# Ordering attention keys by blocks of sixteen heads, most of them inside the first chunk of a graph network on one NeuronCore

## The chip, the cores and the metric

The kernel runs on one core of one Trainium2 chip. The metric is the device time of one execution in microseconds; lower is better. Engines are named as in the profile: PE (matrix products), DVE (vector engine), ACT (activations), POOL (GpSimd), SP (the engine that issues most transfers here). SPq in the profile is SP's queue of transfers.

## The reference

There are N = 3327 nodes with 128 features, a dense weighted adjacency matrix `adj` of 3327 x 3327, and four layers, each a normalisation, a ReLU, a graph layer and a residual sum. The change touches the first layer alone, an attention with 128 heads of 8 elements over all nodes, in which `adj` is added twice to the scores:

```python
q = (x @ Wq.T).reshape(d, n, h)          # d = 128 heads, n = 3327, h = 8
k = (x @ Wk.T).reshape(d, n, h)
v = (x @ Wv.T).reshape(d, n, h)
a = jnp.einsum('dnh,dmh->dnm', q, k) * scale
a = a + spatial_encoding + edge_encoding  # both are adj
a = jax.nn.softmax(a, axis=2)
out = jnp.einsum('dnm,dmh->dnh', a, v)
```

So 128 score matrices of 3327 x 3327 are made, exponentiated and multiplied with the values. The other three layers multiply `adj` and its transpose with 128 features per node.

## The kernel before, in words

**Prologue.** x is normalised and transposed, q, k and v are projected (L345). The raw k goes to `kraw_d`, element by element (eight elements, each for all heads), q split into a high and a low half (fp32r and the rest) to `qS_d`, v to `v_d`. Four "squares" of `adj`, 128 columns each, are turned into `adjT` with the maxima of its rows (class `Square`, L268 and after: `load` reads four strips of rows into the tile `rows`, `turn` transposes them on DVE at L288 into the tile `cols`, `largest` at L292 takes maxima, `store` writes `cols` to `adjT` at L295, `gather` at L299 and `back` at L304 pass the maxima through DRAM, `finish` adds them to the bound).

**Ordering the keys.** `k_halves(e)` (L412) is called eight times among the projections of v (L426 to L436), once for each of the eight elements. It loads element e of all 128 heads (L415), and for even and odd tiles of nodes makes the high half on ACT (L420) and the low half on DVE (L421), reading with a stride of 26 elements, and stores both to `kS_d` (L423). `kS_d` has, for each half, element and head, the nodes in the order in which the attention loop wants its tiles. The prologue is scheduled by the framework; from L599 on, the program's order is each engine's order.

**The attention loop.** There are 7 chunks c of up to 476 queries, 32 groups g of 4 heads in each, and 13 pairs q of node tiles in each group; a pair has the running number u. The order is written out by hand in the loop at L796 in slots i, four for a pair. In a slot stand ACT's exponentials (`exps`, L666 and L669), DVE's seeds of the score banks (`seed`, L645: a tile of `adjT` less the shift is put in a PSUM bank before PE adds the scores of four heads to it one after the other), PE's products (`scores` L654, `values` L713), and, for pairs 0, 2, 5, 7 and 10 of each group, an exponential made on DVE instead of ACT (`hand_exp`, L691 to L697). A score bank becomes free when ACT has read it, and the seed of a pair three or four pairs on waits for that.

Loads for the next group are issued by SP in the program's order: at pair 1 the keys (`load_k`, sixteen transfers into `KT`, L551), the first head's q (`load_q`, L562 and L564) and the values (`load_v`, L575); at pairs 3, 5 and 7 POOL writes the negated q of one head into the next head's rows (`negate_q`, L570) and SP loads the next head's q over a part of it; at pair 8 POOL spreads the values (L580) and reads the keys once (`all_here`, L584), on which the group's first score waits. SP runs ahead of the other engines as far as buffers are free.

Other work is put behind a pair with `plan(u, f, ...)`: in slot 4u, after the first pieces of `hand_exp` and before the seeds and loads of that pair, f issues its instructions. `plan_squares(c)` so spreads the squares of chunk c + 1 over chunk c: one strip in a group, loaded at pair 0, turned at pairs 4 and 9, its maxima at pair 12; each square ends with `gather`, `back`, `finish` and `store` at pairs 0, 1, 7 and 8 of the next group. The tiles `cols` and `rows` have one buffer each.

After the loop the outputs are normalised and projected, and the other three layers follow.

## Time and profile before

| What | us |
|---|---|
| median of 3 runs | 10980.69 (10976.75 to 10984.85) |
| profiled execution | 10981.96 |
| its span | 10980.2 |
| prologue, up to the loop's first instruction | 419.2 |
| first score of the loop (L654) | 461.2 |
| first and last store copy of the loop (L721) | 518.2 and 10170.7 |
| granted TensorE clock over the span | 0.985 |

The profiled execution is 1.3 us above the median. The page gives each engine's busy time over the whole span, which mixes the prologue (0 to 419 us), the loop (to about 10180 us) and the last three layers; what is true of one isn't true of the other. In a timeline row stand the start, the busy time, the engine, the line, the operation, what is written from what is read, the number of instructions merged into the row, and in brackets how long the engine was idle before and who ended it. For SPq a row is the time that issuing took, not that of the transfer; the time to landing has to be read from the engine that waits for it.

### The profile page before, as it was taken

What the parts mean: (1) busy time and instruction counts of PE and PEld (TensorE: products, weight loads), DVE (VectorE), ACT (ScalarE), POOL (GpSimd) and SP (SyncE); (2) the same over time, 40 slices, a digit from 0 to 9 for tenths busy, and PEclk for the clock granted to TensorE, in tenths of its full rate; (3) what the DMA queues carried; (4) which work ended last, traced back from release to release, by engine and by line L of the source; (5) the groups of instructions that cost most, each with busy time, mean ns of one, the idle gap of its engine ahead of it and who ended that gap; (6) DMA issues with size and microseconds to landing.
All of it is one profiled execution on the core that took longest, in us unless ns stands there. A gap on an engine that the chain in (4) does not pass through costs nothing. (4 is left out here: it accounts for less than half of the span.)

```text
span 10980.2 us, 204474 instructions
## 1 busy us (share of the span) xinstructions
PE 10533.5 (96%) x72876; PEld 3435.7 (31%) x72876; DVE 8487.1 (77%) x13503; ACT 10033.1 (91%) x13789; POOL 1529.1 (14%) x2477
## 2 busy tenths in 40 slices
PE   4599999999999999999999999999999999999889
PEld 2133333333333333333333333333323333333544
DVE  5588887888878887788887888878877777777655
ACT  3599999999999999999999999999999999999330
POOL 5011111111111111111111111111111111111101
PEclk7799999999999999999999999999999999999999
DMA  8766566565566565565556565565556555554668
GB/s 250 250 99 97 94 96 113 93 98 96 89 118 97 93 97 88 106 98 97 90 95 119 94 96 93 95 119 95 87 93 98 96 95 86 82 88 71 206 233 281
DMA packets 695339, 1256.98 MB, mean 114 GB/s; under 512 B 195218, under 2 KB 555049, under 8 KB 691244
## 3 DMA queue, kind: packets, MB, share of 16 engines
q1 hardware_dynamic: 644044, 1114.42, 55.7%
q0 software_dynamic: 50272, 129.37, 4.3%
q8 instruction: 587, 9.62, 0.4%
q14 instruction: 436, 3.57, 0.2%
HBM read 1096.53 MB, written 146.60 MB: 113 GB/s over the span
## 5 line engine op out<-in xcount | busy, mean ns | idle before, releaser
L666 ACT ACTIVATE e<-S 128x952 f32<-128x952 f32 (+1 forms) x9024 | 8357.9, 1099 | 36.7 <-PE S L654 29.4
L713 PE MATMUL po<-e,VA 128*9 128x476 f32 (+1 forms) x46592 | 5737.5, 564 | 33.0 <-DVE OS L721 12.3
L645 DVE TENSOR_TENSOR S<-a,shb 128x476 f32<-128x476 f32 (+1 forms) x5824 | 3937.9, 676 | 1447.6 <-ACT e L666 1059.4
L654 PE MATMUL S<-QS,KT 64*128 64x476 f32 (+1 forms) x22176 | 4528.6, 445 | 79.7 <-DMA a<-adjT 28.4
L654 PEld LDWEIGHTS S<-QS,KT 64*128 64x128 f32 x22176 | 2073.7, 184 | 5100.5 <-issue 1301.3
L669 ACT ACTIVATE e<-S 128x476 f32<-128x476 f32 (+1 forms) x4128 | 2467.5, 711 | 1.1 <-PE S L654 0.6
L695 DVE SCALAR_TENSOR_TENSOR e<-e,h 128x476 f32<-128x476 f32 (+1 forms) x2240 | 1497.8, 669 | 77.0
L713 PEld LDWEIGHTS po<-e,VA 128*9 128x9 f32 x46592 | 691.0, 88 | 1606.6 <-issue 1488.1
L570 POOL TENSOR_SCALAR QS<-QS 128x476 fp32r<-128x476 f32 (+1 forms) x672 | 485.6, 723 | 4312.1 <-DMA QS<-qS_d 2612.2
L725 POOL DMA_DIRECT2D oT_d<-OS x896 | 470.5, 530 | 3668.8 <-DVE OS L721 3625.5
L691 DVE TENSOR_SCALAR h<-S 128x476 f32<-128x476 f32 (+1 forms) x1120 | 728.0, 650 | 300.9 <-PE S L654 296.5
L697 DVE SCALAR_TENSOR_TENSOR e<-e,EA 128x476 f32<-128x476 f32 (+1 forms) x1120 | 759.6, 678 | 0.0
L695 DVE SCALAR_TENSOR_TENSOR e<-h 128x476 f32<-128x476 f32 (+1 forms) x1120 | 743.1, 663 | 0.0
L1107 PE MATMUL pu<-strip,y 128*128 128x512 f32 (+2 forms) x1456 | 600.5, 566 | 31.7 <-DVE y L968 14.8
L654 PE MATMUL S<-QZ,KT 64*128 64x476 f32 (+1 forms) x1120 | 493.4, 441 | 11.9 <-DVE S L645 10.5
L1107 PEld LDWEIGHTS pu<-strip,y 128*128 128x128 f32 (+1 forms) x1456 | 271.9, 191 | 305.8 <-issue 272.1
L1111 DVE TENSOR_REDUCE deg<-strip 128x1 f32<-128x1536 f32 (+1 forms) x104 | 193.8, 1881 | 63.7 <-DMA strip<-adjT 44.1
L580 POOL COPY VA<-VR 128x832 f32<-128x832 f32 x224 | 242.3, 1082 | 0.0
L654 PEld LDWEIGHTS S<-QZ,KT 64*128 64x128 f32 x1120 | 205.1, 183 | 92.2 <-DVE S L645 52.4
L288 DVE STREAM_TRANSPOSE cols<-rows 128x416 f32<-128x416 f32 x208 | 204.5, 988 | 30.3 <-DMA rows<-in_adj_dram 22.6
L1060 ACT COPY uT<-pu 128x512 f32<-128x512 f32 (+1 forms) x21 | 11.1, 555 | 222.6 <-PE pu L1107 222.6
L721 DVE COPY OS<-po 128x476 f32<-128x476 f32 (+1 forms) x224 | 146.3, 653 | 87.3 <-PE po L713 87.3
(255 smaller groups left out, 1958.6 us busy)
## 6 DMA issues: line engine op xcount, KB each, us to landing
KT<-kS_d SPq DMA_DIRECT2D x1792, 208.0 KB
KT<-kS_d SPq DMA_DIRECT2D x1792, 104.0 KB
VR<-v_d SPq DMA_DIRECT2D x224, 416.0 KB
QS<-qS_d SPq DMA_DIRECT2D x3072, 14.9 KB
QS<-qS_d SPq DMA_DIRECT2D x1536, 29.8 KB
adjT<-cols SPq DMA_DIRECT2D x26, 1664.0 KB
a<-adjT SPq DMA_DIRECT2D x156, 238.0 KB
strip<-adjT POOLq DMA_DIRECT2D x39, 895.5 KB, 5.1
```

The source lines that it names most:

```text
L570: nc.gpsimd.tensor_scalar(QS[b][:, j + 1, :w], QS[b][:, j, :w].bitcast(F32), -1.0, 0.0, op0=ALU.mult, op1=ALU.add)
L580: nc.gpsimd.tensor_copy(VA[(c * NG + g) % 2][:, :, :, 0:H], v.rearrange("p j (t e) -> p t j e", e=H))
L645: touch(u, [r], nc.vector.tensor_tensor(bank(u, r), adj_of[c][2 * q + r][:, :w], shift_of[c][:, :w], op=ALU.subtract))
L654: x = nc.tensor.matmul(bank(u, r), KT[b][64 * r:64 * r + 64, max(0, j - 1), q * P:(q + 1) * P], q_s[64 * r:64 * r + 64, :w], start=hand an ...
L666: touch(u, (0, 1), nc.scalar.activation(e[:, :, :w], S[:, odd:even + 1, :w], AF.Exp, scale=2.0))
L669: touch(u, [r], nc.scalar.activation(e[:, 1 - r, :w], bank(u, r), AF.Exp, scale=2.0))
L691: touch(u, [1], nc.vector.tensor_scalar(s, bank(u, 1), EXP_ARG, None, op0=ALU.mult))
L695: nc.vector.scalar_tensor_tensor(e, s if k == 3 else e, EXP_C[k], s, op0=ALU.add, op1=ALU.mult)
L697: nc.vector.scalar_tensor_tensor(e, e, EXP_C[0], EA[pairs[u][2]][:, :w], op0=ALU.add, op1=ALU.mult)
L713: nc.tensor.matmul(po[32 * j:32 * j + H + 1, :w], VA[k % 2][:, 2 * pairs[v][2] + of, j, :], e_of[v, j][:, 1 - of, :w], start=(q == 0 and r ...
L725: nc.gpsimd.dma_start(oT_d[:, d * N + c * CW:d * N + c * CW + w], o[32 * j:32 * j + H + 1, :w])
L1107: nc.tensor.matmul(ps[:, :k], y[:m, t, :], s[:m, c * 4 * P - c0:c * 4 * P - c0 + k], start=(t == 0), stop=(t == NT - 1))
```

## The change

Keys are ordered by blocks of 16 heads with all eight elements (16 x 8 = 128 rows) instead of by elements with all heads. Block 0 is ordered in the prologue, at the third pair of value tiles. Blocks 1 to 7 are ordered in the loop's first chunk: block b from the third pair of group 4(b - 1) on; it holds the keys that are loaded from pair 1 of group 4b - 1 on. There the high half is made by DVE and the low half by POOL, a half of the nodes' tiles at a time, in the tiles `cols` and `rows` of the squares. The four squares of chunk 1 move to the second half of these blocks, two strips to a group. Ahead of the loop, the first group's q of all four heads is loaded at once and negated in rows of 32, with the shift and four adj tiles ahead of the keys; values and the other adj tiles come after the keys. (The branch for scores without a bound gets the remaining blocks too; it doesn't run.)

```diff
+    def k_rows(b):
+        return bass.AP(tensor=kraw_d.tensor, offset=kraw_d.offset + KB * b * N, ap=[[N, KB], [GP, H], [1, N]])
...
-            if t0 >= 10:
-                k_halves(t0 // 2 - 5)
+            if t0 == 4:
+                k_block(0, a2)
...
-                if c + 1 < NC and (g, q) == (0, 0):
+                if c and c + 1 < NC and (g, q) == (0, 0):
                     plan_squares(c)
...
+            class Keys:
...
+                def load(self):
+                    raw = e_t.tile([P, NT, P], F32, name="cols").rearrange("p t n -> p (t n)")
+                    nc.gpsimd.memset(raw[:, N:NP], 0.0)
+                    nc.sync.dma_start(raw[:, :N], k_rows(self.b))
+                    self.of = raw.rearrange("d (p q r) -> d r q p", q=NQ, r=2)
+
+                def high(self, r, q0, q1):
+                    self.part = e_t.tile([P, 7 * P], F32, name="rows")[:, :(q1 - q0) * P]
+                    nc.vector.tensor_copy(self.part.rearrange("d (q p) -> d q p", p=P).bitcast(F32R),
+                                          self.of[:, r, q0:q1, :])
+                    k_store(self.b, 0, r, q0, self.part)
+
+                def low(self, r, q0, q1):
+                    part = self.part.rearrange("d (q p) -> d q p", p=P)
+                    nc.gpsimd.tensor_tensor(part.bitcast(F32R), self.of[:, r, q0:q1, :], part, op=ALU.subtract)
+                    k_store(self.b, 1, r, q0, self.part)
+
+            def plan_keys():
+                for b in range(1, HEADS // KB):
+                    u, keys = 4 * (b - 1) * NQ, Keys(b)
+                    plan(u + 2, keys.load)
+                    for at, r, h in ((5, 0, 0), (9, 0, 1), (14, 1, 0), (21, 1, 1)):
+                        plan(u + at, keys.high, r, 7 * h, 7 + 6 * h)
+                        plan(u + at + 2, keys.low, r, 7 * h, 7 + 6 * h)
+                    if b <= squares_of(1) - squares_of(0):
+                        sq = Square(e_t, squares_of(0) + b - 1)
+                        for j in range(4):
+                            v = u + 26 + 6 * j + j // 2
+                            plan(v, sq.load, j)
+                            plan(v + 3, sq.turn, j, 0)
+                            plan(v + 5, sq.turn, j, 1)
+                            plan(v + 5, sq.largest, j)
+                        for k, f in ((25, sq.gather), (25, sq.store), (27, sq.back), (33, sq.finish)):
+                            plan(u + 26 + k, f)
...
-            v0 = load_v(0, 0)
-            load_k(0, 0)
-            load_q(0, 0, 0)
-            shift_of[0] = load_shift(0)
-            for j in range(3):
-                negate_q(0, 0, j)
-                load_q(0, 0, j + 1)
+            for j in range(4):
+                load_q(0, 0, j)
+            shift_of[0] = load_shift(0)
+            adj_of[0] = [load_adj(0, t) for t in range(4)]
+            load_k(0, 0)
+            v0 = load_v(0, 0)
+            adj_of[0] += [load_adj(0, t) for t in range(4, NT)]
+            for j in range(3):
+                for r0 in (32 * (1 - j % 2), 64 + 32 * (1 - j % 2)):
+                    nc.gpsimd.tensor_scalar(QS[0][r0:r0 + 32, j + 1, :CW], QS[0][r0:r0 + 32, j, :CW].bitcast(F32),
+                                            -1.0, 0.0, op0=ALU.mult, op1=ALU.add)
             spread_v(0, 0, v0)
             here[0] = all_here(0, 0)
-            adj_of[0] = [load_adj(0, t) for t in range(NT)]
```

`k_block(b, pool)`, used for block 0, does what `k_halves` did, with `k_rows(b)` as its source; `k_store` writes the sixteen heads' rows of one half into `kS_d`.

More of the change, by code (lines that the diff above doesn't have):

```diff
@@ L39 @@
 NG = HEADS // 4
+KB = P // H
 HALF_SCALE = 0.5 * D ** -0.5
@@ L275, in load @@
                 self.cols = self.pool.tile([P, NT, P], F32, name="cols")
-            self.rows = self.pool.tile([P, KW], F32, name="rows")
+            self.rows = self.pool.tile([P, 7 * P], F32, name="rows")[:, :KW]
             n0 = self.s * P + 32 * j
@@ L320, in square, with k_store, k_block @@
         return q
+    def k_rows(b):
+        return bass.AP(tensor=kraw_d.tensor, offset=kraw_d.offset + KB * b * N, ap=[[N, KB], [GP, H], [1, N]])
+    def k_store(b, i, r, q0, half):
+        m = half.shape[-1]
+        nc.sync.dma_start(bass.AP(
+            tensor=kS_d.tensor, offset=kS_d.offset + (i * H * HEADS + KB * b) * NP + (r * NQ + q0) * P,
+            ap=[[NP, KB], [HEADS * NP, H], [1, m]]), half)
+    def k_block(b, pool):
+        raw = pool.tile([P, NP], F32, name="st_q0")
+        nc.gpsimd.memset(raw[:, N:NP], 0.0)
+        nc.sync.dma_start(raw[:, :N], k_rows(b))
+        of = raw.rearrange("d (p q r) -> d r q p", q=NQ, r=2)
+        for r in range(2):
+            hi = pool.tile([P, NQ, P], F32R, name="st_k0")
+            lo = pool.tile([P, NQ, P], F32R, name="st_q1")
+            nc.scalar.copy(hi, of[:, r])
+            nc.vector.tensor_tensor(lo, of[:, r], hi.bitcast(F32), op=ALU.subtract)
+            for i, half in enumerate((hi, lo)):
+                k_store(b, i, r, 0, half.bitcast(F32).rearrange("d q p -> d (q p)"))
     def head_rows(tensor):
@@ L410, in bound_scores @@
             return wide
-        def k_halves(e):
-            raw = a2.tile([P, NP], F32, name="st_q0")
-            nc.gpsimd.memset(raw[:, N:NP], 0.0)
-            nc.sync.dma_start(raw[:, :N], head_rows(kraw_d[e]))
-            of = raw.rearrange("d (p q r) -> d r q p", q=NQ, r=2)
-            for r in range(2):
-                hi = a2.tile([P, NQ, P], F32R, name="st_k0")
-                lo = a2.tile([P, NQ, P], F32R, name="st_q1")
-                nc.scalar.copy(hi, of[:, r])
-                nc.vector.tensor_tensor(lo, of[:, r], hi.bitcast(F32), op=ALU.subtract)
-                for i, half in enumerate((hi, lo)):
-                    nc.sync.dma_start(kS_d[i, e, :, r * NQ * P:(r + 1) * NQ * P],
-                                      half.bitcast(F32).rearrange("d q p -> d (q p)"))
         v_rows = v_d.rearrange("(p t) d -> p t d", t=NT)
@@ L460, in gnn_kernel @@
                 square(d2, s, d2)
+            for b in range(1, HEADS // KB):
+                k_block(b, d1)
             for t in range(NT):
@@ L756, in plan, with __init__ @@
                 behind.setdefault(u, []).append((f, a))
+            class Keys:
+                def __init__(self, b):
+                    self.b = b
+                def load(self):
+                    raw = e_t.tile([P, NT, P], F32, name="cols").rearrange("p t n -> p (t n)")
+                    nc.gpsimd.memset(raw[:, N:NP], 0.0)
+                    nc.sync.dma_start(raw[:, :N], k_rows(self.b))
[10 more added lines that the diff above has]
+            def plan_keys():
+                for b in range(1, HEADS // KB):
+                    u, keys = 4 * (b - 1) * NQ, Keys(b)
[13 more added lines that the diff above has]
+                            plan(u + 26 + k, f)
             def plan_squares(c):
@@ L788, in gnn_kernel @@
             bare(0, 0)
+            plan_keys()
             def in_slot(i):
```

## The prediction

> **What bounds the kernel now.** I read the page first: the span, the busy times, the costliest groups (here the seeds on DVE, with mean ns and the idle time before them).
>
> ```profile
> span 10980.2 us, 204474 instructions
> PE 10533.5 (96%) x72876; PEld 3435.7 (31%) x72876; DVE 8487.1 (77%) x13503; ACT 10033.1 (91%) x13789; POOL 1529.1 (14%) x2477
> ...
> L645 DVE TENSOR_TENSOR S<-a,shb 128x476 f32<-128x476 f32 (+1 forms) x5824 | 3937.9, 676 | 1447.6 <-ACT e L666 1059.4
> ```
>
> Then the busy times by stage: from 500 to 1900 us, in 1400 us, ACT has 1396.2 and PE 1386.4, DVE 1134.8. The attention loop (224 groups of 13 pairs, one group each 43.2 us by the stores' copies at 604.66, 648.15 and 691.30) is filled by ACT and PE, so only a hole in it costs time. DVE is 81% busy, but it seeds the banks that PE and ACT need next: if it stops, they stop a little later. Before the loop lies a prologue up to 419.2 us, in which the DMA share is 0.90 to 0.99 from 50 to 400 us.
>
> **What the change takes from the prologue.** Eight orderings of keys (each 1.66 MB loaded, four stores of 0.83 MB) become one. The last of them:
>
> ```profile
> 365.90 6.58 ACT L420 CAST st_k<-st_q 128x1664 fp32r<-128x1664 f32 x2 [11.87 <-DMA st_q<-kraw_d]
> 372.74 3.36 ACT L420 CAST st_k<-st_q 128x1664 fp32r<-128x1664 f32 x1 [0.27 <-DMA kS_d<-st_k]
> ...
> 406.72 3.36 ACT L420 CAST st_k<-st_q 128x1664 fp32r<-128x1664 f32 x1 [2.04 <-DMA kS_d<-st_k]
> ```
>
> The last key store is issued at 413.4 and the loop starts at 419.2. The values, which go on beside the keys, have their 13 stores at 277.5 to 351.6, 6.2 us apart. Without seven eighths of 40 MB beside them the spacing falls: not below the 3.70 us of a pair's eight matmuls, not above 6.2. I take 4.3, nearer the matmuls: last store at 277.5 + 12 x 4.3 = 329, some 7 us to land (9.4 is the page's median, beside the keys), the loop at 336: **83 us won** (58 if the values keep their pace: 352 + 9.4; 90 at 3.7).
>
> **The first loads.** Today: keys issued from 420.3 to 437.0, then q and negations by turns to 456, adj behind them, first scores 461.2, 41.4 us after the first issue. New order: 27 q loads (0.36 us each, 10 us), shift and four adj tiles (3 us), then the keys. The sixteen key transfers keep the DMA engines full at 128 GB/s (425 to 437 us), about 20 us for 2.5 MB. Then values, 4 us. So 38 to 39 us: **2 us won** (0 to 8). The six short negations lie under the key transfer.
>
> **What it puts into the loop.** Seven blocks, each a load of 1.66 MB, four DVE copies, four POOL subtractions, eight stores of about 0.45 MB, through SP's one queue. What counts is that queue's order. A block's load is planned two pairs into a group, so it stands behind that group's sixteen key loads, its first q and its values; the first DVE copy, which needs it, is planned at pair 5. Where SP and DVE stand in such a group today:
>
> ```profile
> 638.55 12.62 SPq L551 DMA_DIRECT2D KT<-kS_d  x16
> ...
> 660.57 0.39 SPq L575 DMA_DIRECT2D VR<-v_d  x1
> ```
>
> ```profile
> 655.56 0.65 DVE L691 TENSOR_SCALAR h<-S 128x476 f32<-128x476 f32 x1 [0.59 <-PE S L654]
> 656.24 2.20 DVE L645 TENSOR_TENSOR S<-a,shb 128x476 f32<-128x476 f32 x3
> ```
>
> L691 at 655.56 is pair 5's, the seed after it ends at 656.9, and the copy would come there. But SP issues the values only at 660.57, and the load after that. The load takes about 8 us: issued at 357.82, used at 365.90. So DVE waits D + 0.8 + 8 - 1.4, D being the values' issue less pair 5's start: here 5.0, in the group at 768 us (no rows ahead of its keys) 787.85 - 785.10 = 2.75, in the group at 725 us, with a square's 1.66 MB store beside the keys, 753.14 - 741.82 = 11.3, in the first group 491.20 - 480.3 = 10.9.
>
> What such a wait costs, the trace of before shows once, in chunk 5:
>
> ```profile
> 8187.84 0.65 DVE L697 SCALAR_TENSOR_TENSOR e<-e,EA 128x476 f32<-128x476 f32 x1
> 8197.41 0.95 DVE L288 STREAM_TRANSPOSE cols<-rows 128x416 f32<-128x416 f32 x1 [8.93 <-DMA rows<-in_adj_dram]
> ```
>
> ```profile
> 8201.22 0.97 ACT L666 ACTIVATE e<-S 128x952 f32<-128x952 f32 x1 [7.72 <-PE S L654]
> ```
>
> The copy of that group's store comes at 8183.4, the next at 8236.1: 52.7 us against 43.2. A wait of 8.93 us cost 9.5. Price: the wait plus 0.6.
>
> Here the skill can be weighed. The granted clock is 1.00 up to 8196, 0.66 from 8196 to 8200, 0.50 to 8204, then 0.99: the stop also slowed PE for some 7 us, and the 0.6 holds that. The Trainium skill ("TensorE: Matmul & The Clock Gate", What's actually happening) says that PE falls to half its clock after an idle window of about 3.4 us and needs as much activity to come back. An estimate from this page charges each of 22 stalls up to 3.4 us instead of 0.6, 62 us more in all, and would make the time 11158; the row charges 0.6, because ACT and not PE alone fills a group, and the row decides.
>
> The stalls, one by one:
>
> - **The block's load, seven times.** Block 1: D is 10.9 less some 3 for the earlier loads, wait 15.4. Blocks 2 to 5 follow a square whose maxima, read-back and store now all come just ahead of the keys: D 12, wait 19.4. Blocks 6 and 7: D 2.75, wait 10.2. With 0.6 and 0.9 for the copy itself: 16.9 + 4 x 20.9 + 2 x 11.7 = **124 us** (96 if the load lands in 4 us instead of 8, the 0.6 being kept; 145 at 11).
> - **The fourth copy, seven times.** The store at pair 14 waits for DVE and stands ahead of the second group's keys: these start about 5.7 us later than at 638.55, the values at 666.3. The low half's store of pair 16 is behind them; 0.83 MB landed 3.5 to 5.2 us after issue (369.24 to 372.74, 401.57 to 406.72), so this lands near 671. The copy at pair 21 needs the same buffer at pair 8 of that group, 662.02 + 3.3 = 665.3. 5.5 us each, **38 us** (14 to 55).
> - **Rows of the squares, eight times.** Two of four strips are now loaded at pair 6 and turned at pair 9. SP reaches pair 6 behind the third q, at 669.2, issues four loads in 1.7 us, and they land 2 to 3 us later, 673.5; the turn came at 669.4. 3.5 us each, **28 us** (8 to 40).
> - **The copies and POOL.** The trace has no DVE copy with this stride. L421, with it, took 3.32 us for 1664, so 1.8 us for 896; a plain seed has 1.42 ns an element, 1.3 us. A turn of 0.99 us costs nothing today: groups with turns take 43.2 like the others. The 0.8 above it, for the copies that needn't wait, and POOL beside DVE (two seeds took 1.84 instead of 1.42 us beside L570): **10 us** (0 to 25).
>
> A subtraction on POOL: L369 has 1.27 us for 512, so 2.2 for 896, between a store of 3.5 us and the next; 9.2 of the 12.4 us between pairs 5 and 9, so no stall. The Trainium skill ("GPSIMD Engine Reference", Performance pitfalls for Q7 kernels) has half as much again for reads at strides over 8 bytes; an estimate by that is 3.3 us, 10.3 of 12.4, also none. No row shows this form.
>
> The squares' work itself is only moved; it was free, and the DMA share of 0.60 from 500 to 1900 us has room for 35 MB. Oddly placed, not too much, is the trouble: each transfer is late for one in-order engine.
>
> **Sum.** Won 83 + 2 = 85; lost 124 + 38 + 28 + 10 = 200. Net 115 us slower. The profiled execution took 10981.96 us (1.8 outside its span), 1.3 above the median of 10980.69; 10982 + 115 = 11097, and to compare with the median **11096**.
>
> **Rivals.**
>
> - **Faster: the loads are there in time.** One mechanism: if the block's load overtook the key transfers or SP ran further ahead than it does, DVE would not wait at pair 5, and what stays is 85 less the 10 for copies and a few late buffers: 10905 to 10930. It decides where the seven stalls average below 85 / 7 = 12 us with nothing else lost. For it: SP does issue keys a little ahead of a group (766.89 against 768.3), and the DMA share falls to 0.12 late in a group (668 to 681 us). Against it: the values are issued after pair 5 in all four groups above. 0.14.
> - **About even.** Load waits at their lower end (96), buffers hardly late (14 + 8): 118 - 85 = 33 us slower, and with 1 us less at each of 22 stops, where DVE's lead covers it, 11 us: 10992. That is within 0.2% (22 us, about what a measurement of this kernel can tell from no change). 0.06.
> - **The prologue doesn't get shorter as said**: the values keep their pace, 58 won, all else the same: 11121. 0.15.
> - **Worse**: every term at its upper end, 145 + 55 + 40 + 25 - 85 = 180: 11161. 0.15.
> - The forecast itself, all between 11020 and 11110: 0.50.
>
> So slower 0.80, same 0.06, faster 0.14. The range leaves out the faster case, and takes in the even one below and the worst above: 10985 to 11165.
>
> **What would show it.** Loop start at 336 instead of 419. In the first chunk, DVE waits before the new key copies, on the DMA of the block's load, 10 to 20 us each, seven times, with ACT idle 8 to 20 us after them and the clock falling to 0.5; waits of about 5 us before every fourth copy; waits before turns at pair 9. Groups of 43 us from chunk 1 on, as before. Wrong would be: copies with no DMA wait ahead of them, the block's load issued before the keys, or groups of 44 us throughout chunk 0.

## The result, and the profile after

The changed kernel takes 11187.08 us (median of 4 runs, 11182.35 to 11189.40), the kernel before 10981.08 in the same comparison: a ratio of 1.0187, with a 95% interval of 1.0174 to 1.0199. It is 206 us slower. The forecast was 115 us slower, 11096 us, with a range up to 11165: the direction held, the size did not.

The page of the changed kernel, the same three rows as before (busy time and share, then the seeds with their sum, mean ns and idle time):

```profile
span 11187.3 us, 204548 instructions
PE 10597.9 (95%) x72876; PEld 3446.8 (31%) x72876; DVE 8515.0 (76%) x13517; ACT 9999.8 (89%) x13775; POOL 1604.6 (14%) x2508
...
L657 DVE TENSOR_TENSOR S<-a,shb 128x476 f32<-128x476 f32 (+1 forms) x5824 | 3943.0, 677 | 1451.8 <-ACT e L678 1061.2
```

The engines do the same work (ACT 10033 us before, 9999.8 now; PE 10533 and 10598), and the seeds cost the same. What is longer is the span. So it is holes, and the next step is to find where. I measure with one mark: the first instruction of an exponential by hand (L691 before, L703 after), which DVE issues at pairs 0, 2, 5, 7 and 10 of each group.

| Stretch, us | before | after |
|---|---|---|
| up to pair 0 of the first group | 462.9 | 379.8 |
| first chunk (32 groups) | 1387.5 | 1685.4 |
| the other six chunks, up to pair 0 of the last group | 8270.8 | 8265.4 |
| from there to the end | 859.0 | 856.7 |

83 us are won ahead of the loop, as forecast, and 298 are lost in the first chunk, where 200 were forecast. The later chunks are as before, to 5 us in 8270. The five segments between the marks show where in a group the 298 us lie:

| Part of the first chunk, us lost | forecast | after |
|---|---|---|
| first group of a block, pairs 5 to 7 (the load) | 124 | 155 |
| first group, pairs 7 to 10 (blocks 2 to 5) | 0 | 21 |
| second group of a block | 38, at pair 8 | 57, of which 49 at pairs 0 to 5 |
| squares' groups | 28 | 52 |
| copies and POOL, and the rest | 10 | 12 |

SP's timeline in the first group of block 2 (start, busy time, line, operation):

```profile
629.80 0.39 SPq L587 DMA_DIRECT2D VR<-v_d  x1
630.24 0.57 SPq L778 DMA_DIRECT2D cols<-kraw_d  x1
...
643.49 0.57 SPq L329 DMA_DIRECT2D kS_d<-rows  x1
...
652.35 0.36 SPq L311 DMA_DIRECT2D bound_d<-b  x1
652.80 0.57 SPq L329 DMA_DIRECT2D kS_d<-rows  x1
```

DVE's timeline beside it (in brackets the idle time before, and who ended it):

```profile
618.93 0.65 DVE L703 TENSOR_SCALAR h<-S 128x476 f32<-128x476 f32 x1 [0.60 <-PE S L666]
...
641.62 1.84 DVE L783 CAST rows<-cols 128x896 fp32r<-128x896 f32 x1 [21.34 <-DMA cols<-kraw_d]
...
663.57 0.89 DVE L783 CAST rows<-cols 128x768 fp32r<-128x768 f32 x1 [6.08 <-DMA kS_d<-rows]
```

Both stops can be read off. The values come out of SP's queue 10.9 us after pair 5's start, the load behind them at 630.24, and it is used at 641.62: 11.4 us from issue to use, 21.3 us of idle DVE. The second copy then waits 6.1 us for its buffer: the low half's store was issued at 652.80, right behind that of the row bounds. SP's waits around that store in the whole run (us in total, times, longest):

```profile
SPq L311 <- DVE b L310: 20.3, 4, 5.2
SPq L329 <- DMA bound_d<-b: 17.6, 4, 4.7
```

SP stands some 5 us until DVE has the row bounds of pair 7, then issues their store, 128 pieces of four bytes, and then the low half's. By the trace's records of landings, the bounds' store landed 8.3 to 9.0 us after its issue, in all four blocks that have one, and the low half's store right behind it 10.6 to 11.1 us after its own; every other key store in this kernel's loop landed 3.3 to 4.7 us after its issue.

What DVE's stop does to the others, by stages (window and its length, then PE, PEld, DVE, ACT and POOL busy, granted clock, DMA share, GB/s):

```profile
632.00:636.00 4.00, 0.00 (x0) 0.00 (x0) 0.00 (x0) 0.00 (x0) 0.00 (x0) 0.50 1.16 283
636.00:640.00 4.00, 0.00 (x0) 0.00 (x0) 0.00 (x0) 0.00 (x0) 0.00 (x0) 0.50 0.96 206
640.00:644.00 4.00, 0.00 (x0) 0.00 (x0) 2.38 (x2) 0.00 (x0) 0.58 (x1) 0.50 0.24 42
644.00:648.00 4.00, 3.91 (x19) 1.16 (x22) 3.78 (x7) 2.13 (x3) 0.70 (x1) 0.50 0.62 149
648.00:652.00 4.00, 4.00 (x26) 0.99 (x24) 1.70 (x4) 3.18 (x5) 4.00 (x3) 0.79 0.01 0
```

For more than twelve microseconds PE, ACT and DVE compute nothing; the clock is at 0.50 and stays there until 649.7, 5.6 us after PE has gone on at 644.1. While the load runs alone the DMA share is about 1 and only 206 GB/s are moved: the transfer engines are full (14.6 rows in flight at a time), and slow.

In the second group of a block there is no such wait, but this (all engines, after the start of group 6):

```profile
688.41 0.65 DVE L707 SCALAR_TENSOR_TENSOR e<-h 128x476 f32<-128x476 f32 x1
...
689.10 4.41 DVE L707 SCALAR_TENSOR_TENSOR e<-e,h 128x476 f32<-128x476 f32 x2
...
690.36 2.62 POOL L789 TENSOR_TENSOR rows<-cols,rows 128x896 fp32r<-128x896 f32 x1
...
694.93 0.57 ACT L681 ACTIVATE e<-S 128x476 f32<-128x476 f32 x1 [3.22 <-PE S L666]
```

Two instructions of 0.67 us took 4.41 us together, one of them 3.72, while POOL subtracted. ACT stood still for 3.22 us behind them. DVE was not waiting there; it was busy, and slow.

### The profile page after: what moved, and what is told of

It is laid out like the page before. It is cut to its first block, busy times and chain, and to the rows that moved or that the text cites. A ratio compares the mean times of both kernels' runs of the same rounds, so it can differ in the third digit from the quotient of the medians.

```text
span 11187.3 us, 204548 instructions
## 1 busy us (share of the span) xinstructions
PE 10597.9 (95%) x72876; PEld 3446.8 (31%) x72876; DVE 8515.0 (76%) x13517; ACT 9999.8 (89%) x13775; POOL 1604.6 (14%) x2508
## 5 line engine op out<-in xcount | busy, mean ns | idle before, releaser
L657 DVE TENSOR_TENSOR S<-a,shb 128x476 f32<-128x476 f32 (+1 forms) x5824 | 3943.0, 677 | 1451.8 <-ACT e L678 1061.2
L707 DVE SCALAR_TENSOR_TENSOR e<-e,h 128x476 f32<-128x476 f32 (+1 forms) x2240 | 1523.5, 680 | 77.0
L703 DVE TENSOR_SCALAR h<-S 128x476 f32<-128x476 f32 (+1 forms) x1120 | 727.9, 650 | 345.1 <-PE S L666 339.7
L709 DVE SCALAR_TENSOR_TENSOR e<-e,EA 128x476 f32<-128x476 f32 (+1 forms) x1120 | 763.9, 682 | 0.0
L707 DVE SCALAR_TENSOR_TENSOR e<-h 128x476 f32<-128x476 f32 (+1 forms) x1120 | 746.5, 667 | 0.0
L1117 ACT COPY uT<-pu 128x512 f32<-128x512 f32 (+1 forms) x21 | 11.1, 552 | 222.4 <-PE pu L1164 222.4
## 6 DMA issues: line engine op xcount, KB each, us to landing
QS<-qS_d SPq DMA_DIRECT2D x3072, 14.9 KB
```

The lines of the kernel that those rows point to most:

```text
L657: touch(u, [r], nc.vector.tensor_tensor(bank(u, r), adj_of[c][2 * q + r][:, :w], shift_of[c][:, :w], op=ALU.subtract))
L703: touch(u, [1], nc.vector.tensor_scalar(s, bank(u, 1), EXP_ARG, None, op0=ALU.mult))
L707: nc.vector.scalar_tensor_tensor(e, s if k == 3 else e, EXP_C[k], s, op0=ALU.add, op1=ALU.mult)
L709: nc.vector.scalar_tensor_tensor(e, e, EXP_C[0], EA[pairs[u][2]][:, :w], op0=ALU.add, op1=ALU.mult)
```

## The experiments

Each kernel was timed against the kernel before on the same chip. Edits are against the changed kernel if nothing else is said. My theory: the prologue's gain is real, and the loop loses by late transfers on SP's in-order queue (load, low half's store, rows), plus POOL's hold on DVE. The rivals: the work itself (copies on DVE) costs, or the load is late for another reason.

### The gain alone

```diff
-            plan_keys()
...
-                if c and c + 1 < NC and (g, q) == (0, 0):
+                if c + 1 < NC and (g, q) == (0, 0):
...
-                    k_d = kS_d[:, :, d, r * NQ * P:(r + 1) * NQ * P]...
+                    k_d = kS_d[:, :, d % KB, r * NQ * P:(r + 1) * NQ * P]...
```

> Leaves out the ordering of blocks 1 to 7 in the loop: every group reads the keys of the first 16 heads instead, and chunk 1's squares are back at their old places. What is left of the change is the short prologue and the new order of the first loads. Both theories (late transfers on SP's queue; POOL holding DVE) put the whole loss into the blocks in the loop: 10981 - 83 = 10898, by the 83 us by which pair 0's L703 of the changed kernel comes before L691 of the kernel before (379.8 against 462.9). A rival, that the new prologue itself does harm in the loop (keys read in another place, q loaded otherwise), expects groups longer than 43.2 us and over 10920.

10891.7 us, ratio 0.9918 (0.9901 to 0.9934). First chunk 1386.7 us, against 1387.5 before, first mark at 375.7. Blocks 1 to 7 are left out. What the change wins ahead of the loop is as forecast; all else is lost in the first chunk.

### The low halves on DVE

```diff
-                    nc.gpsimd.tensor_tensor(part.bitcast(F32R), self.of[:, r, q0:q1, :], part, op=ALU.subtract)
+                    nc.vector.tensor_tensor(part.bitcast(F32R), self.of[:, r, q0:q1, :], part, op=ALU.subtract)
```

> The subtraction of the low halves moves from POOL to DVE, nothing else. If POOL's subtraction holds DVE while it runs (in the changed kernel an instruction of 0.67 us takes up to 3.72 beside it, 52 us in all over 28 subtractions), this ends; DVE gets 28 instructions of 1.5 to 1.9 us in their place, which partly fit into gaps: 30 to 70 us faster than 11187, so 11120 to 11157, and the 5.8 us between pairs 2 and 5 of every block's second group are gone. If POOL does no harm, and only SP's queue makes transfers late, DVE just has 45 us more to do: 11190 to 11230.

11207.45 us, ratio 1.0206 (1.0189 to 1.0223). The time is the rival's, but the trace says why both were too simple. At pairs 2 to 5 of the second groups the loss fell from 4.6–5.9 to 1.7–1.9 us (3.4 twice): POOL's hold was there and is gone. The subtraction works in place, though, and must let the high half's store finish reading. POOL waited for that beside everybody; now DVE does (the waits of DVE, us in total, times, longest):

```profile
DVE rows L783 <- DMA kS_d<-rows: 32.3, 11, 4.5
DVE rows L789 <- DMA kS_d<-rows: 27.2, 7, 6.3
```

So an experiment on one cause put a new wait in its place.

### The blocks' transfers on POOL's queue

```diff
-                    nc.sync.dma_start(raw[:, :N], k_rows(self.b))
+                    nc.gpsimd.dma_start(raw[:, :N], k_rows(self.b))
...
-                    k_store(self.b, 0, r, q0, self.part)
+                    k_store(self.b, 0, r, q0, self.part, nc.gpsimd)
...
-                    k_store(self.b, 1, r, q0, self.part)
+                    k_store(self.b, 1, r, q0, self.part, nc.gpsimd)
```

> The blocks' loads and stores in the loop are issued by POOL instead of SP, at the same places of the program. If SP's order makes them late (the load is issued at 20 to 30 us of a group and lands 11 to 12 us later), the load is now issued at 6 us, or for blocks 2 to 5 when the square's store has landed, about 10, and shares the DMA engines with the keys: it lands at 20 to 26, DVE waits 2 to 8 us instead of 13 to 22, and the stalls before the second copies of blocks 2 to 5 go as well: 90 to 150 us faster, 11040 to 11100. If the DMA engines are the limit, because the key transfers fill them, the load lands after them whatever its queue, at 28 or later: at most 40 us faster, 11150 or more. POOL's hold on DVE stays in both.

11095.69 us, ratio 1.0106 (1.0089 to 1.0123): 91 us won by taking these transfers off SP's queue. That is a net figure, since pairs 7 to 10 of the blocks' first groups now lose 50 us instead of 21. The stop at pairs 5 to 7 fell to 0.7–1.5 us in blocks 1, 6 and 7. Blocks 2 to 5 kept 12 to 18 us: their load needs the tile that a square's store still reads, and POOL, now in order behind that, waited 70.8 us in three waits.

### The load two pairs earlier

```diff
-                    plan(u + 2, keys.load)
+                    plan(u, keys.load)
```

> The block's load is planned at pair 0 instead of pair 2, so that SP issues it ahead of the group's key loads. By the theory of SP's order, DVE's wait at pair 5 is gone for blocks 1, 6 and 7 (20 us each); for blocks 2 to 5 SP now waits for the square's store ahead of the keys, the load lands at some 22, and the keys come 10 us later: 10 to 15 us less each: 11070 to 11120. If the load is slow for a reason of its own (12 us beside anything), it still lands before pair 5 in blocks 1, 6 and 7, and the time is the same; if the waits at pair 5 came from elsewhere, nothing changes: 11180 or more.

11141.06 us, ratio 1.0143 (1.0126 to 1.0160): 46 us won, between the two cases. The stop at pairs 5 to 7 went (1 to 7 us left), but pairs 7 to 10 of blocks 2 to 5 lost 22 to 24 us each. DVE's waits:

```profile
DVE rows L783 <- DMA kS_d<-rows: 98.1, 9, 24.9
```

Now the low half's store stands behind the next group's keys, q and values, and the second copy waits for its buffer. Moving one transfer ahead only hands the lateness to the next.

### Rows adjacent in DRAM

```diff
-                    nc.sync.dma_start(raw[:, :N], k_rows(self.b))
+                    nc.sync.dma_start(raw[:, :N], head_rows(kraw_d[self.b]))
```

> The block's load reads 128 rows that lie one behind the other in DRAM, in place of sixteen heads' rows taken element by element over all of it; bytes, rows and queue are the same, and the keys come out in a wrong order. If the order of the rows in DRAM is what makes the load land 11.5 us after its issue (and not 8), each of the seven stops at pairs 5 to 7 gets 3 to 4 us shorter: 11155 to 11170 us, with the load landing 7.5 to 8.5 us after its issue. If it is slow because it shares the transfers with the next group's keys, q and values, which stand ahead of it on SP, nothing changes: 11180 to 11195 us, landing 11 to 13 us after the issue.

11154.36 us, ratio 1.0158 (1.0141 to 1.0175). The same first group of block 2, SP and DVE:

```profile
615.91 0.50 SPq L778 DMA_DIRECT2D cols<-kraw_d  x1
...
623.50 1.85 DVE L783 CAST rows<-cols 128x896 fp32r<-128x896 f32 x1 [17.91 <-DMA cols<-kraw_d]
```

The load was issued at 615.91: 7.6 us instead of 11.4. A row of 13308 bytes took a transfer engine 0.50 us instead of 0.95, and the load ran at some 360 GB/s instead of 200. Same bytes, same queue, same neighbours: the order of the rows is what made it slow.

### The bounds' store later

```diff
-                        for k, f in ((25, sq.gather), (25, sq.store), (27, sq.back), (33, sq.finish)):
+                        for k, f in ((25, sq.gather), (25, sq.store), (27, sq.back), (36, sq.finish)):
```

> The changed kernel with the squares' last step (finish, which issues the store of the row bounds) three pairs later, at pair 10 instead of pair 7. If the low half's first store waits on SP behind that store at pair 7, and the second copy for it, the 5.1 to 5.6 us at pairs 7 to 10 of blocks 2 to 5 go: 11160 to 11172 us. If the low store is late anyway because of the next group's loads ahead of it, 11180 to 11190 us.

11159.26 us, ratio 1.0161 (1.0146 to 1.0177). The first group of block 2, SP:

```profile
635.50 0.57 SPq L329 DMA_DIRECT2D kS_d<-rows  x1
...
641.94 0.56 SPq L329 DMA_DIRECT2D kS_d<-rows  x1
...
650.86 0.54 SPq L329 DMA_DIRECT2D kS_d<-rows  x1
...
654.10 0.36 SPq L311 DMA_DIRECT2D bound_d<-b  x1
```

```profile
649.90 0.94 DVE L783 CAST rows<-cols 128x768 fp32r<-128x768 f32 x1
```

The low half's store comes 6.4 us after the high half's instead of 9.3, and lands 3.7 us after its issue instead of 10.7; DVE's wait of 6 us ahead of the second copy (649.90) is gone. The loss at pairs 7 to 10 of blocks 2 to 5 fell from 21 to 1.5 us. So 128 row bounds of four bytes, three pairs too early, cost 20 of the 28 us; the other 8 are spread over the stretches, 5 of them ahead of the loop, where the two kernels do not differ.

### The squares alone

```diff
-                    plan(u + 2, keys.load)
...
-                        plan(u + at, keys.high, r, 7 * h, 7 + 6 * h)
-                        plan(u + at + 2, keys.low, r, 7 * h, 7 + 6 * h)
```

(and all groups read the first sixteen heads' keys)

> Blocks 1 to 7 are not ordered in the loop (no load, no copy, no subtraction, no store; all groups read the keys of the first sixteen heads); the squares stay where the change puts them. Against the prologue alone (10891.7 us) the difference is the squares' new order. If the 53 us that the squares' groups lost come from that order itself (denser turns, rows loaded at pair 6), about 10945 us (10930 to 10955). If they come from the keys' stores and tiles in the same groups, 10895 to 10920 us.

10925.32 us, ratio 0.9948 (0.9931 to 0.9965), 33.6 us above the gain alone, between the two cases. So the squares' denser order costs 33 us by itself, near the 28 forecast, but spread over the pairs of turns and maxima: DVE's waits for rows are 8.5 us of it, three waits of at most 3.0. The other 20 of the 52 come with the keys: the changed kernel's first strip waits on SP for the last low half's store, which reads the tile `rows`, and the second strip's rows (issued at 762.59 for the second square) came late, so that its turn waited 6.4 to 7.8 us in each square. Here that turn does not wait.

### POOL's subtraction alone

```diff
-                    nc.sync.dma_start(raw[:, :N], k_rows(self.b))
...
-                    nc.vector.tensor_copy(self.part.rearrange("d (q p) -> d q p", p=P).bitcast(F32R),
-                                          self.of[:, r, q0:q1, :])
-                    k_store(self.b, 0, r, q0, self.part)
+                    nc.gpsimd.memset(self.part, 0.0)
...
-                    k_store(self.b, 1, r, q0, self.part)
```

(in `load` POOL fills the whole tile `cols` instead, and all groups read the first sixteen heads' keys)

> As the squares alone, and in addition POOL's 28 subtractions at their pairs, on tiles that POOL itself has filled with zeros: no load, no copy on VectorE, no store. If POOL's subtraction holds VectorE (an operation of 0.67 us beside it took 3.72 us in the changed kernel), each holds it by about 2 us, and most of that shows where no stop hides it: 35 to 60 us over the squares alone. If the subtraction is hidden and what the second groups lost is the copy on VectorE, 0 to 10 us over the squares alone.

10998.60 us, ratio 1.0015 (1.0006 to 1.0025): 73 us above the squares alone, more than the 35 to 60 expected (the 28 fills of `rows` on POOL, 0.73 to 0.85 us each, and seven of `cols`, 2.9 us each, are in it too). One of the second groups, at pairs 2 to 5:

```profile
433.69 4.41 DVE L707 SCALAR_TENSOR_TENSOR e<-e,h 128x476 f32<-128x476 f32 x2
...
434.97 2.62 POOL L786 TENSOR_TENSOR rows<-cols,rows 128x896 fp32r<-128x896 f32 x1
```

No copy, load or store of a block is left, and the second groups still lose 4.6 to 5.9 us at pairs 2 to 5. That loss is POOL's.

### A spread order of seven blocks

```diff
-                    u, keys = 4 * (b - 1) * NQ, Keys(b)
-                    plan(u + 2, keys.load)
+                    u, keys = 3 * (b - 1) * NQ, Keys(b)
+                    plan(u + 8, keys.load)
...
+                        for h, at, put_hi, put_lo in ((0, 5, 6, 8), (1, 11, 13, 13)):
...
+                            plan(v + at, keys.high, r, q0, q1)
+                            plan(v + at + 1, keys.low, r, q0, q0, q0 + 4)
+                            plan(v + at + 2, keys.low, r, q0, q0 + 4, q1)
+                            plan(v + put_hi, keys.put, 0, r, q0, q1)
+                            plan(v + put_lo, keys.put, 1, r, q0, q1)
```

> The same keys and squares in another order: three groups for a block, its load issued at pair 8 behind the next group's last q, copies and subtractions all on VectorE in pieces of one to six q, a tile of its own for the low half, so that nothing is changed in place while a store reads it, stores issued at pairs 6, 8 and 13, the squares of the second chunk in the last ten groups of the first, and 26 adjacency tiles instead of 28 to make room. If the 298 us of the first chunk are the stops for loads and stores on SP's queue and POOL's hold on VectorE, and not the work itself, nearly all of it goes: 10900 to 10945 us, under the kernel before. If the work on VectorE is what costs (about 13 us of it for a block), 10960 to 11060 us.

10992.96 us, ratio 1.0011 (1.0002 to 1.0021): 194 us under the changed kernel, and still not under the kernel before. The number is in the range of the second case, but not for its reason: groups 0 to 21, which hold the keys, lost 32 us in all, with 1.2 us of DVE's waits on a block's load or stores. The last ten groups, eight of them with two strips of squares, lost 57 us (SP's timeline in one of them):

```profile
1455.32 3.48 SPq L300 DMA_DIRECT2D rowmax_d<-rm  x4
1458.84 5.30 SPq L284 DMA_DIRECT2D rows<-in_adj_dram  x4
1465.32 13.23 SPq L563 DMA_DIRECT2D KT<-kS_d  x16
...
1495.64 1.91 SPq L284 DMA_DIRECT2D rows<-in_adj_dram  x4
```

Maxima and rows stand ahead of the next group's keys, everything behind is late, and the strip's turn waited 7.07 us. In later chunks the group before each change of chunk took 47 to 48.6 us, where the kernel before took 44.6 to 45.0: 26 adjacency tiles are one chunk's worth, with none to spare.

### Five blocks in the loop, low halves on DVE or POOL

```diff
-            if t0 == 4:
-                k_block(0, a2)
+            if t0 in (4, 8, 12):
+                k_block(t0 // 4 - 1, a2)
...
-                for b in range(1, HEADS // KB):
+                for b in range(3, HEADS // KB):
```

and the squares one strip a group from group 15 on; in the second kernel the subtraction is POOL's. In both, one strip of the last square is turned in part from the rows of the strip after it.

> Three blocks ordered ahead of the loop, five in it by the spread order (three groups each, groups 0 to 14), and the second chunk's squares at one strip a group in groups 15 to 29, as wide apart as in the kernel before. In the spread order of seven blocks the groups of keys lost 5.5 us a block and the squares, packed two strips to a group, some 55 us. If the packed strips (SP's queue held by their rows and by the stores of the row bounds) are the cause, they cost at most 10 us here: 10891.7 + 2 x 12.7 for the two blocks ahead of the loop + 5 x 5.5 + 10, so 10945 to 10965 us, under the kernel before. If 26 adjacency tiles or the squares as such are the cause, it stays within 10975 to 11000 us.

> As the spread order of five blocks, with the low halves subtracted by POOL in one piece in place of VectorE in two pieces, into the same tile of their own. VectorE has about 1.8 us less to do for each of the 20 low halves. If POOL's subtraction holds VectorE for most of its 2.6 us, and sets VectorE back at pairs where it has no slack, 2 to 4 us a subtraction: 30 to 70 us slower than with VectorE. If POOL works beside VectorE and the hold is hidden, 10 to 30 us faster than with VectorE.

10985.62 us, ratio 0.9999 (0.9990 to 1.0008), and 10986.45 us, 1.0005 (0.9996 to 1.0014). No gain, and the first is where its second case has it. Squares at one strip a group cost next to nothing (most groups 42.9 to 43.2 us; the one with two strips 52.2), and the keys 4.4 us a block. A block ahead of the loop cost 14.9 us and not 12.7 (first mark 405.4), but that is 4 us in all. Of the rest, 25 us lie in the later chunks, most of it at their changes: the group before a change took 46.0 to 50.5 us. The kernels further down that have 28 adjacency tiles again take 44.4 to 45.5 there from the second change on, so this is the price of 26 tiles. Between the two kernels there is no difference in the time, which neither case of the second had: in the 15 groups with keys they lost 22 us with DVE's subtractions and 29 with POOL's. With time for it, POOL's hold costs DVE about as much as the subtraction itself would.

### All blocks ahead of the loop

```diff
-            if t0 == 4:
-                k_block(0, a2)
+            if 4 <= t0 < 20:
+                k_block(t0 // 2 - 2, a2)
```

and the squares as in the kernel before, nothing of the keys in the loop.

> All eight blocks of keys ordered ahead of the loop by blocks of sixteen heads, the squares as in the kernel before, the first group's loads as in the changed kernel. From the kernel before this differs by the first loads and by the blocks' form (rows taken element by element over sixteen heads). If the loads of the first group are worth the 9 us that the trace shows and a block ahead of the loop costs the same in either form (12.7 us), 10965 to 10975 us. If the sixteen-head blocks load slower ahead of the loop too (3.5 us each, as in the loop), 10990 to 11000 us.

11017.71 us, ratio 1.0031 (1.0020 to 1.0043), beyond both cases. The first mark is at 496.1 us, 17.2 us for each of seven blocks; the kernel before paid (462.9 - 8.3 - 375.7) / 7 = 11.3, with 8.3 for the first loads. So a block of sixteen heads is dearer than an element of all heads wherever it is done.

### The rows in another order

```diff
-        return bass.AP(..., ap=[[N, KB], [GP, H], [1, N]])
+        return bass.AP(..., ap=[[GP, H], [N, KB], [1, N]])
...
-            ap=[[NP, KB], [HEADS * NP, H], [1, m]]), half)
+            ap=[[HEADS * NP, H], [NP, KB], [1, m]]), half)
```

once in the changed kernel, once with all blocks ahead of the loop.

> The changed kernel with the partitions of a block in another order: the sixteen heads of one element of the head lie on partitions one behind the other, so that sixteen rows in a row are adjacent in DRAM, in place of eight elements of one head, whose rows lie 512 rows' stride or more apart. Same bytes, same result, loads and stores alike. If the jump from row to row is what slows the load, it lands about 8 us after its issue as with adjacent rows, and stores gain a little: 11145 to 11165 us. If only 128 rows in one piece are fast, 11180 to 11190 us.

> All eight blocks ahead of the loop, with the same other order of partitions. With the change's order these eight cost 17.4 us each of the loop's start (496.1 us against 374.6 with one block), where the kernel before paid 11.3 for its form. If the jump from row to row is the cause, they go back to about 11.3 us each, 43 us for the seven: 10970 to 10980 us. If it is the smaller pieces of the stores or the order of the blocks, 11010 to 11020 us.

11288.92 us, ratio 1.0276 (1.0260 to 1.0292), and 11094.48 us, 1.0096 (1.0081 to 1.0112). Sixteen adjacent rows in a row should have helped; it got 102 and 77 us worse. The load of block 2 in the loop:

```profile
652.33 0.67 SPq L778 DMA_DIRECT2D cols<-kraw_d  x1
...
670.62 1.84 DVE L783 CAST rows<-cols 128x896 fp32r<-128x896 f32 x1 [28.95 <-DMA cols<-kraw_d]
```

Issued at 652.33, it took 18.3 us. While it ran alone (same columns as above):

```profile
654.00:670.00 16.00, 0.00 (x0) 0.00 (x0) 0.00 (x0) 0.00 (x0) 0.00 (x0) 0.50 0.56 130
```

The DMA share is 0.56, not 1: counting the rows in flight, 7.7 at a time here, 14.6 in the changed kernel, and 14 with adjacent rows. About half the transfer engines stood idle. The Trainium skill ("DMA: Bandwidth & Descriptors", Why a DMA increments its semaphore by 16 and not by 1) gives the rule: a transfer runs on the largest number of engines up to 16 that divides the slowest dimension of both its patterns. Here that dimension is 8 where the change has 16, and 7.7 in flight agrees. My theory of the jumps is not confirmed by this: in the loop a row still took 0.92 us. Ahead of the loop, rows in the same order took 0.92 in the first two blocks and 0.50 to 0.53 in the other six. Why a row takes 0.95 us in the change's order stays open (ahead of the loop it took 0.66 to 0.98 in this order); that in the loop it does, and that 128 rows in one piece take 0.50, is shown.

### Three orders that avoid what was found

```diff
+            lows = [e_adj.tile([P, CW], F32, name="a") for _ in range(2)] + [e_t.tile([P, P], F32, name="low")]
...
-                    plan(u + 2, keys.load)
+                    plan(u - 0, keys.load) if u else keys.load()
```

The low halves lie in two adjacency tiles that the first chunk has to spare (28 tiles again) and a small one. The second part of the diff is the third kernel's. The first kernel has the other row order; the next two have the change's order.

> Four blocks ahead of the loop and four in it, three groups each in groups 0 to 11, in the other order of partitions; copies and subtractions on VectorE in pieces, the low halves in two adjacency tiles that nobody needs in the first chunk and a small one (28 adjacency tiles as before); the squares at one strip a group in groups 13 to 28. Loop's start 374.6 + 3 x 11.3 = 408.5 us instead of 462.9; first chunk 1387.5 + 4 x 5 + 2: 32 us under the kernel before, 10945 to 10960 us. If the jump is not what slows the blocks, the three ahead of the loop cost 17.4 each: 10963 to 10978 us. If the squares or the spread keys cost as such, 10980 us or more.

> The change's own order of partitions; three blocks ahead of the loop, five in it, three groups apart, the first of them loaded ahead of the loop and each other one five pairs ahead of its first copy's group; copies and subtractions on VectorE in pieces, low halves in two adjacency tiles that the first chunk does not need (28 as before); squares one strip a group in groups 14 to 29. Loop's start 405.4 us as in the five-block run (462.9 before); first chunk 1387.5 + 5 x 4.8 + 4 for the squares' last steps; later chunks as before. 57.5 won, 28 lost: 10945 to 10962 us. If the low halves in three stores or the load in front of a group cost another few us a block, 10965 to 10985 us.

> The same with one block ahead of the loop and seven in it, two groups apart (groups 0 to 13), each load issued on SP right behind the last store of the block before, five or six pairs ahead of the copy. Loop's start 375 us, first chunk 1387.5 + 7 x 4.8 + 4: 88 won and 38 lost, 10925 to 10945 us, if the load lands 12 us after its issue and before the copy at pair 6, and if the next group's keys, which then stand behind it on SP, still land in time. If they come too late or the copy waits, 5 to 10 us a block: 10965 to 11005 us.

11056.83 us, ratio 1.0068 (1.0054 to 1.0082) for the first, beyond all its cases: its blocks ahead of the loop cost 30.5 us each (mark at 467.2), and its first chunk lost 61 us. Then 10972.23 us, 0.9989 (0.9980 to 0.9998), and 10969.17 us, 0.9986 (0.9977 to 0.9995): both a little faster than before, and both where the second case of their expectations had them. The seven-block order wins 88.3 us ahead of the loop and loses 68.3 in the first chunk, 4.8 to 8.2 of it at pairs 10 to 13 of each of five even groups. One of SP's waits from 460 to 540 us in that kernel:

```profile
SPq L563 <- DMA cols<-kraw_d: 8.7, 1, 8.7
```

Before one of the next group's key transfers SP waits for the landing of the block's load, and the high half's store, far behind, is late for the second copy (DVE idle 3.35 us for its buffer; 21.0 us in six such waits).

```diff
-                    nc.sync.dma_start(raw[:, :N], k_rows(self.b))
+                    nc.gpsimd.dma_start(raw[:, :N], k_rows(self.b))
```

> The seven blocks two groups apart, with only the blocks' loads issued on POOL's queue instead of SP's. In the run before, the even groups lost 5 to 8 us at pairs 10 to 13: SP stood 8.7 us behind the block's load before the next group's keys, the high half's store came out of the queue at 39 instead of 33 us into the group, and the second copy waited for it. If SP's order is the cause, these 5 us go in six groups: 10935 to 10955 us. If the keys' transfers themselves are slowed by sharing the engines with the load, or POOL's issue of 128 rows holds VectorE, 10962 to 10985 us.

10960.30 us, ratio 0.9979 (0.9969 to 0.9988), 23 us faster than the kernel before, the best version found. First mark 376.3, first chunk 1451.5 us. The wait on the load is gone from SP, but four even groups still lose 4.7 to 7.8 us at pairs 10 to 13, and one of them had lost 1.0 there before. DVE's waits for the high half's buffer fell only from 21.0 to 14.9 us. The last key transfer still leaves SP 21 to 25 us into an even group (28 in the first), against 15 in an odd one: SP now waits for the keys' own transfers (18.4 us in the same stretch, 10.7 before), so the shared engines are the likely rest, which no further run tested.

## Why the prediction was wrong

**Right.** What bounds the kernel, and that only holes cost. The prologue: 85 us forecast for loop start and first loads together, 83.0 measured at the first mark (86 to 89 in the other runs with the same beginning). That the sum fits is luck: the loop's first instruction came at 344.5 instead of 336 (75 won, not 83; the values' stores are 3.43 us apart at the end, not 4.3, but start later), and the first loads were worth 8.3 us, not 2. The stops at pair 5, their cause (SP's queue) and their number are as told. So is the forecast that it is slower.

**Wrong.** The loss in the first chunk, 298 us against 200. Of the 98 us beyond the forecast, the block's load has 31, the second groups 19, a stop that was not foreseen 21, the squares 24; the rest is 2 or 3.

**The block's load, 124 forecast, 155 measured.** The failed term is the 8 us to landing, taken from loads of 128 adjacent rows. In the change's row order it is 11.3 to 12.8 us (adjacent rows: 7.6 again, and 33 us back). My upper end of 11 us was too low. The waits add up to 131.9 us (seven, on the load) where I had 113.4. The price behind a wait was 3.3 us and not 1.5: 1.8 of it is the copy, which I had charged at 0.9 beyond what is free, and 1.5 is left, which I had at 0.6 from a stop of 9 us. The slow clock is the likely rest, not measured by itself: these stops are 14 to 22 us long, and PE runs at 0.50 for 3.6 to 6.0 us after it goes on. The estimate by the Trainium skill ("TensorE: Matmul & The Clock Gate", What's actually happening), up to 3.4 us for each, was at least 1.9 us too high; the row was up to 0.9 too low.

**The fourth copy, 38 forecast, 57 in the same groups.** The mechanism was not the one named. At pairs 7 to 10 only 0.2 to 1.1 us were lost; the fourth copies had no wait for the store. What costs is POOL's subtraction. I had looked at its own duration (2.2 us forecast, 2.26 to 3.13 measured) and asked whether it ends before the next copy, and had 10 us for everything it does to DVE. Beside the 28 subtractions DVE's instructions were stretched by some 53 us in sum, and at pairs 2 to 5 that shows: 4.6 to 5.9 us, seven times.

**Not foreseen, 21 us.** I wrote that POOL's work between pairs 5 and 9 makes no stall. I counted POOL's 9.2 of 12.4 us, with 3.5 us for a store to land, and left out whom the low half's store stands behind on SP: `finish` of the last square, at the same pair. Behind that it landed 10.6 to 11.1 us after its issue. My text said that what counts is SP's order, and at this place I did not look at it.

**The squares, 28 forecast, 52 measured.** The order itself is 33.6 us. That this is near 28 is luck: the waits for rows, which made up the 28, are 8.5 us of it, and the rest lies at the pairs of the turns and maxima, which I had at nothing. The rest comes with the keys beside it: the waits for the second strip's rows, 27 us in four, are absent where the keys are left out.

**Where the chances went.** "Worse" had every term at its upper end and 0.15; it was 11161, and three terms lie beyond their upper ends, and 21 us are in none. The bounds came from rows of another form: a load in another order, a seed beside a light POOL instruction.

## What to carry to other kernels

Work that is moved off the start of a kernel into a loop must be priced by its transfers' places in each in-order queue, and by every buffer that their landing frees; removing one late transfer mostly shows the next. A transfer's time is not its bytes: which rows lie adjacent, and how many rows the outermost dimension has, changed the same 128 rows of 13308 bytes (1.70 MB) from 7.6 to 18.3 us from issue to use. A small store is not small for what stands behind it: 128 pieces of four bytes made the next store land 7 us later. And an engine that is idle is not free to use, if another has to stand still while it works.

## What was not expected of the hardware

- The same 1.70 MB in 128 rows of 13308 bytes, in the loop: about 360 GB/s with 128 adjacent rows, 200 with eight elements of each of sixteen heads in turn, 112 with sixteen heads of each of eight elements.
- 128 pieces of four bytes, one from each partition, landed 8.3 to 9.0 us after their issue, and a key store issued 0.45 us behind them 10.6 to 11.1 us after its own, four times out of four; the other key stores in the loop took 3.3 to 4.7 us.
- A DVE instruction with two operands in SBUF took up to 3.72 us instead of 0.65 beside a POOL subtraction of 2.62 us: so the polynomial's steps (L707, up to 3.72 us), its last step (L709, 3.10) and seeds (L657, 2.72). Those that were held end 0.51 to 0.52 us after the subtraction. Step L703, which reads a PSUM bank alone, kept its 0.65 us in the four places where it ran beside one, two of them wholly within it. The Trainium skill ("SBUF — State Buffer", Who interferes with whom) says that a VectorE instruction with two inputs in SBUF and a GpSimd instruction that reads SBUF exclude each other, and that the one that comes later stands still. The trace agrees that they exclude each other; four places are few for L703. Who comes first the recorded starts do not tell: the instructions of 3.72 us start 0.58 us ahead of POOL's and still wait for its end.
- A strided copy on DVE took 1.88 us for 896 elements (7 x 128) and 0.95 for 768 (6 x 128).
